# Layer 0 of a four-layer convolution kernel: C spread over the partitions through DRAM, and some events moved to other ticks

## The chip, the core and the metric

The kernel runs on one core of one Trainium2 chip. A core has five engines, each with an instruction stream of its own that it works through in order: TensorE (PE in the profile; PEld are its weight loads), VectorE (DVE), ScalarE (ACT), GpSimd (POOL) and SyncE (SP, which here only issues DMAs). The metric is the device time of one execution in microseconds.

## The reference, cut to what matters

`x` is 8 images of 128 channels and 64 x 64 pixels. Four layers follow, each as `x = x + layer(group_norm(x))`. Only layer 0 is touched. Its upper 64 channels go through a 3 x 3 convolution, its lower 64 through a selective scan over the 4096 pixels of an image:

```
t  = (x_id @ expand_w) @ concat_w + concat_b            # 64 channels
xz = layer_norm(t) @ in_w + in_b;  xs, z = split(xz)    # 128 channels each
xc = silu(causal_conv1d(xs))
dbc = xc @ xproj_w                                      # 4 + 16 + 16 columns
dt = softplus(dbc[:R] @ dt_w + dt_b); B, C = dbc[R:R+16], dbc[R+16:]
h  = exp(dt * A) * h + dt * B * xc                      # scan; h has 128 x 16 states
y  = (sum over the 16 states of h * C + xc * D) * silu(z)
x_id_out = t + y @ out_w + out_b
x = x + relu(concat(x_id_out, conv3x3(x_hw) + conv_b))
```

Layer 1 (`propagate`) is a chain of four directions with 63 steps each, in which a row is added to a 9-tap convolution of the row before. Layers 2 and 3 are a gated convolution and a deformable convolution.

## The kernel before

**Chunks and steps.** `layer0` (L176 on) cuts the 8 images into 32 chunks `c` of 1024 pixels, four an image, and each chunk into two halves `h` of `T` = 512 pixels. A half is scanned in 8 steps `q`, each for 16 of the 128 channels times 8 states, so that a step fills the 128 partitions; the other 8 states are a second column block `k`. There are 512 steps, and the loop over them makes one *tick* a step. In tick i, POOL weighs the step before (`step_weigh`, L771: `carry` L774 and `hb * C` L775), ACT makes the decay of step i + 2 (`da`, L752), DVE makes `ub = u * B` (L760) and the two scans (L769), SP issues the spreads of `u` for step i + 3 and of `dt` for step i + 5 (`u_s`, `dt_s`, L746), and at i % 4 = 1 PE sums four weighed steps over their states (`round_sum`, L784). `da`, `u_s` and `dt_s` have three buffers each, `hb` seven.

**The order of the rest is written out by hand.** `plan_chunk(c)` puts each further operation of a chunk into a tick counted from the chunk's first step, `t0 = 16 c`, with `at` (after the step's own work) or `ahead` (before it). Each engine executes what falls to it in just this order: tick by tick, and within a tick in the order in which the events were planned, lower chunks first. PE's results of this kind share one ring of two PSUM banks (`ps_g`); B has one pair of banks (`B_ps`).

The operations that matter below, with their lines: `t_product` (L448) and `t_var` (L456); `xs_product` (L478), `z_product` (L493); `v_product` (L504) for each half, with ACT's `e` and `rv`; `v_store` (L531), which stores `dt` and `u` to DRAM, from where L746 spreads them; `bc_product` (L535), with a copy by ACT into `bc` (L537); `spread` (L541), a product with a 0/1 matrix that copies 8 rows of `bc` to all 128 partitions, used by `c_spread` (C, then copied by ACT to SBUF at L549) and `b_spread` (B, left in PSUM); `y_product` (L605 and L607, with ACT's L609), the layer's output product; `normalize` (L570), `conv_taps` (L587), the 3 x 3 convolution of the chunk. For the images 4 to 7 this convolution is computed ahead, in the first half of the chunks, with `early_load` (L633), `early_norm` (L639), `conv_taps` into `ps_e`, `early_relu` (L643) and `early_store` (L646) into the DRAM tiles `cd`; `early` shares the single buffer of `bc`. `norm_at` (L325 to L342) takes an image's statistics through two small products, `ps_gn` and `ps_gv`; `norm_x` (L627) normalises an image of layer 1's input in place; `fold` (L404, L408) folds a norm into two biases.

**What runs beside.** From tick 0 on, `borders` (L170, L176) writes zero borders of eight tables, one DMA a tick in the first 64 ticks. From tick `READY` = 282 (c = 17, tick 10 of the chunk) on, each tick also takes one step of `propagate` for the images 0 to 3: nine taps on PE (`ps_l`, L913) and one operation of DVE (L920). From there on the chunks have `beside` set (c > 16), which places a few events differently. When layer 0 has ended, the rest of the propagation runs alone, then `exchange`, and then layers 1 (images 4 to 7), 2 and 3 beside one another.

Of the kernel before, what the change touches and what calls it, by code (L numbers as in the profile page):

```python
# [10 lines left out]
F32 = mybir.dt.float32  # L11
# [6 lines left out]
P = 128  # L18
B, C, H, W = 8, 128, 64, 64
HW = H * W  # L20
NB2 = B // 2

GC, D, DI, N, R, KC = 64, 64, 128, 16, 4, 3
T = 512
# [16 lines left out]
def conv_preact_kernel(ctx: ExitStack, tc: tile.TileContext, a: dict, out: bass.AP):  # L41
    nc = tc.nc
# [4 lines left out]
    dram = ctx.enter_context(tc.tile_pool(name="dram", bufs=1, space=DRAM))  # L47
# [9 lines left out]
        out=gview, in_=gview, pattern=[[-4, 32], [0, 4]], compare_op=ALU.is_ge,  # L57
# [3 lines left out]
        out=gview, in_=gview, pattern=[[4, 32], [0, 4]], compare_op=ALU.is_ge,  # L61
# [8 lines left out]
    x3d = [dram.tile([C, HW], F32, name=f"x3d{b}") for b in range(B)]  # L70
    cd = [dram.tile([P, T], F32, name=f"cd{c}") for c in range(B * HW // (4 * T))]
    wide = {
        name: [dram.tile([P, T], F32, name=f"{name}_{i}") for i in range(B * HW // T)] for name in ("dtd", "ud")
    }
    tables = [dram.tile([SIDE * DEEP, 2 * C], F32, name=f"table{b}") for b in range(B)]

# [1 line left out]
    norm1 = const.tile([P, B, 2], F32, name="norm1")  # L78
    norm2 = {}
    with tc.tile_pool(name="x", bufs=1) as xp, tc.tile_pool(name="l1w", bufs=1) as wd, tc.tile_pool(  # L80
        name="l1ps", bufs=1, space=PSUM
# [15 lines left out]
        st = const.tile([P, B * NCH, 6], F32, name="bn_st")  # L97
        with tc.tile_pool(name="l2w", bufs=1) as wp, tc.tile_pool(name="l2", bufs=2) as w2, tc.tile_pool(
            name="l3", bufs=2
        ) as w3, tc.tile_pool(name="l2ps", bufs=2, space=PSUM) as p2, tc.tile_pool(  # L100
            name="l3ps", bufs=3, space=PSUM
# [23 lines left out]
            for b in range(B):  # L125
                for when, what in sorted(two.plan(b).items()):
                    n = b * two.TICKS + when
                    if b == NB2:
                        n = (b + 1) * two.TICKS - (two.TICKS - 5 - when) // 2
                    plans.setdefault(n, []).extend(what)  # L130
            last = NB2 * two.TICKS + 30
            for n in range(min(plans), (B + 1) * two.TICKS):
                b, i = n // two.TICKS - 1, n % two.TICKS
# [46 lines left out]
def layer0(tc, a, ident, gmat, x_in, x1d, cd, wide, norm1, X, pl):  # L180


    nc = tc.nc
# [3 lines left out]
    with ExitStack() as ctx:  # L187
# [15 lines left out]
        for i in range(4):  # L203
            part = slice(i * HW // 4, (i + 1) * HW // 4)
# [7 lines left out]
        xproj_w = load("xproj_w", [DI, R + 2 * N], (ALL, a["xproj_w"]), pool=tp)  # L212
# [24 lines left out]
        with tc.manual_schedule():  # L237
# [4 lines left out]
            def ps_g(name):  # L242
                return pg.tile([P, T], F32, tag="g", name=name)
# [8 lines left out]
            ps = ps_g("ps_ec")  # L252
# [8 lines left out]
            ps = ps_g("ps_cb")  # L261
# [5 lines left out]
            ps = ps_g("ps_ib")  # L267
# [13 lines left out]
            for i in (1, 2):  # L281
# [3 lines left out]
            ps = ps_g("ps_dt")  # L285
# [3 lines left out]

            w_bc = wp.tile([DI, 4, 32], F32, name="w_bc")  # L290
            nc.gpsimd.memset(w_bc, 0.0)
            nc.vector.tensor_copy(
                w_bc[:, 0:2, 0:8], xproj_w[:, R + N : R + 2 * N].rearrange("p (k n) -> p k n", n=8)
            )
            nc.vector.tensor_copy(w_bc[:, 2:4, 0:8], xproj_w[:, R : R + N].rearrange("p (k n) -> p k n", n=8))
            w_bc = w_bc.rearrange("p j n -> p (j n)")
            n_of = tp.tile([P, 32], F32, name="n_of")
            nc.vector.tensor_copy(n_of, ident[:, 0:32])
            for j in range(1, 4):
# [8 lines left out]
                out=m_y, in_=m_y, pattern=[[128, 2], [-8, 32]], compare_op=ALU.is_ge,  # L308
# [3 lines left out]
                out=m_y, in_=m_y, pattern=[[-128, 2], [8, 32]], compare_op=ALU.is_ge,  # L312
# [4 lines left out]
            w2 = ctx.enter_context(tc.tile_pool(name="l0", bufs=2))  # L317

            def norm_at(when, st, gm, rs, name):

                box = {}

                def gather():
                    mv = box["mv"] = w2.tile([P, 2], F32, name=f"mv_{name}")
                    nc.vector.bn_aggr(mv, st().rearrange("p a s -> p (a s)"))  # L325

                def mean():
                    mv = box["mv"]
                    ps = ps_g("ps_gn")
                    nc.tensor.matmul(ps[:, 0:1], lhsT=gmat, rhs=mv[:, 0:1], start=True, stop=True)  # L330
                    nc.vector.tensor_copy(gm, ps[:, 0:1])
                    dm = box["dm"] = w2.tile([P, 3], F32, name=f"{name}_dm")
                    nc.vector.tensor_sub(dm[:, 0:1], mv[:, 0:1], gm)
                    nc.vector.scalar_tensor_tensor(
                        dm[:, 1:2], dm[:, 0:1], dm[:, 0:1], mv[:, 1:2], ALU.mult, ALU.add
                    )

                def variance():
                    dm = box["dm"]
                    ps = ps_g("ps_gv")  # L340
                    nc.tensor.matmul(ps[:, 0:1], lhsT=gmat, rhs=dm[:, 1:2], start=True, stop=True)
                    nc.vector.tensor_copy(dm[:, 2:3], ps[:, 0:1])  # L342
                    variances.append((dm[:, 2:3], rs))

                for i, f in enumerate((gather, mean, variance)):
                    at(when + i, f)
# [6 lines left out]
            norm0 = {}  # L353
# [16 lines left out]
            def at(when, what):  # L370
                events.setdefault(when, []).append(what)
# [56 lines left out]
            def plan_chunk(c):  # L428
                b, g = c // NCK, c % NCK
                r0 = g * CR  # L430
                t0 = 16 * c
                s = S[c] = {}
# [4 lines left out]
                n0 = norm0.setdefault(b, {})  # L437
# [101 lines left out]
                def spread(h, j, to):  # L539
                    rows = slice(32 * j, 32 * j + 32)  # L540
                    nc.tensor.matmul(to, lhsT=m_bc[rows], rhs=s["bc", h][rows], start=True, stop=True)  # L541

                def c_spread(h):
                    s["C", h] = w2.tile([P, 2, T], F32, name="C")
                    ps = [ps_g("ps_C") for _ in range(2)]
                    for k in range(2):
                        spread(h, k, ps[k])
                    for k in range(2):
                        nc.scalar.copy(s["C", h][:, k], ps[k])  # L549

                def b_spread(h):
                    s["B", h] = pu.tile([P, 2, T], F32, name="B_ps")
# [43 lines left out]
                                s["res"][HI, h], s["ps_c"][sl], AF.Relu, bias=conv_b[sl]  # L596
                            )

                def y_product():
                    n0 = norm0[b]  # L600
                    s["res"] = w2.tile([P, 2, T], F32, name="res", bufs=1)
                    ps = ps_g("ps_o")
                    x = s["xr"][LO, 1 : 1 + CR, :].rearrange("p (h r) w -> p h (r w)", h=2)
                    for h, sl in enumerate((LO, HI)):
                        nc.tensor.matmul(ps[sl], lhsT=n0["ec"][:, 0, :], rhs=x[:, h], start=True, stop=False)  # L605
                    for h, sl in enumerate((LO, HI)):
                        nc.tensor.matmul(ps[sl], lhsT=out_w, rhs=s["y", h], start=False, stop=True)  # L607
                    for h, sl in enumerate((LO, HI)):
                        nc.scalar.activation(s["res"][LO, h], ps[sl], AF.Relu, bias=n0["ec", "b"][sl])  # L609
# [19 lines left out]
                early = {}  # L629
# [9 lines left out]
                    nc.scalar.activation(v, v, AF.Identity, bias=n1["shift"][HI], scale=n1["rs"][HI])  # L639

                def early_relu():
                    early["out"] = w2.tile([P, T], F32, tag="bc", name="early", bufs=1)
                    nc.scalar.activation(early["out"], early["ps_c"], AF.Relu, bias=conv_b)  # L643

                def early_store():
# [17 lines left out]
                def also(f, *args):  # L663
                    return lambda: f(*args)
# [4 lines left out]
                beside = c > total // 2  # L669
# [20 lines left out]
                    at(t0 - 5, z_product)  # L690
                    at(t0 - 5, exps)
                for h in range(2):
                    at(t0 - 18 + (2 if beside else 1) * h, also(v_product, h))
                    for part in range(2):
                        when = t0 - (14 if c == h == 0 else 10) + 6 * h + part
                        at(when, also(v_sum, h, part))
                        at(when + 2, also(v_store, ("dt", "u")[part], h))
                    lead = 12 if c == h == 0 else 0
                    at(t0 - 3 - beside + 8 * h - lead, also(bc_product, h))
                    at(t0 - 1 + 8 * h - lead, also(c_spread, h))  # L700
                    (ahead if beside else at)(t0 + (0 if beside else -1) + 8 * h - lead, also(b_spread, h))
                    at(t0 + 11 + 8 * h, also(y_gate, h))
                at(t0 + 14, also(y_mul, 0))
# [2 lines left out]
                at(t0 - (14 if c else 16), v_round)  # L706
                at(t0 - (12 if c else 15), v_log)
                at(t0 + 14, load_again)
                at(t0 + 22, y_product)
                if b < NB2:  # L710
                    at(t0 + 20, normalize)
                    for j in range(3):
                        at(t0 + 24 + j, also(conv_taps, taps[3 * j : 3 * j + 3]))
                    at(t0 + 27, early_load)
                    at(t0 + 30, early_norm)
                    for j, ks in enumerate((taps[0:3], taps[3:5], taps[5:7], taps[7:9])):
                        at(t0 + 31 + j, also(conv_taps, ks, r0, early))
                    at(t0 + 34, early_relu)
                    at(t0 + 35, early_store)
                else:  # L720
                    at(t0 + 22, conv_load)
                at(t0 + 27, out_add)
# [2 lines left out]
                if b < NB2:  # L725
                    at(t0 + 30, keep_x)
                if g == NCK - 1:
                    norm_at(t0 + 32, lambda: s["st"], norm1[:, b, 0:1], norm1[:, b, 1:2], "n1")
                    if b < NB2:
                        for part in range(4):  # L730
                            at(t0 + 38 + part, also(norm_x, part))


            def where(i):
# [57 lines left out]
            for c in range(total):  # L792
                plan_chunk(c)
                if c % NCK == 0:
                    b = c // NCK
# [636 lines left out]
```

## Time and profile before

| | before |
|---|---|
| three runs, median (lowest to highest) | 6828.69 us (6819.01 to 6831.93) |
| the profiled execution: time, span | 6825.9 us, 6824.2 us |
| mean granted PE clock | 0.877 |
| busy PE, DVE, ACT, POOL | 81%, 62%, 44%, 64% |
| first scan step; propagation begins; layer 0's steps end; propagation of images 0 to 3 ends | 83, 1390, 2617, 2737 us |
| ticks 0 to 281: PE, DVE, ACT, POOL busy of 1300 us | 1010, 1132, 904, 989 us |
| then to 2611 us: of 1221 us | 1198, 953, 589, 787 us |
| 128 copies of C by ACT (L549) | 586 ns each |
| DMA queue q1 (hardware_dynamic) | 300000 packets, 561 MB, 26.9% of 16 engines |

A line of a group or of a timeline names the line of the code, the engine, the operation, and what it writes and reads by the program's names. What stands in brackets at the end of a timeline line is how long the engine was idle before it and what ended that wait. Times in a timeline begin with the start of the span.

### The profile page before, as it was taken

The numbers are of one execution on the slowest core, as the hardware profiler recorded it, in microseconds if no ns is written. First come the engines' busy times: TensorE is split into PE (matmuls) and PEld (weight loads), VectorE is DVE, ScalarE is ACT, GpSimd is POOL, SyncE is SP. The second block draws the span as 40 slices with busy tenths as digits, with TensorE's granted clock in tenths as the row PEclk, the third lists the DMA queues.
The fourth block names the chain that finished last, engine by engine and source line by source line (L and its number), as shares of the span: only waits on it lengthen the run. The fifth ranks groups of instructions, "written<-read, shape, count | busy, mean of one in ns | idle before, by whom it ended". The sixth has DMA issues, their size and how long they took to land. (4 is left out here: it accounts for less than half of the span.)

```text
span 6824.2 us, 76741 instructions
## 1 busy us (share of the span) xinstructions
PE 5519.9 (81%) x25628; PEld 3703.4 (54%) x25628; DVE 4206.7 (62%) x4615; ACT 3000.8 (44%) x5976; POOL 4342.3 (64%) x3758
## 2 busy tenths in 40 slices
PE   4778887799999999899989999977777777876670
PEld 1222222267676767667777777765645555555550
DVE  4889898877777773427677677766542343433235
ACT  4667777655454541313333333333433343433332
POOL 3778787766666662116776776787666666666655
PEclk7777677799999999899999999998888888987775
DMA  4556565544444441525666666667776666676658
GB/s 123 167 173 190 152 182 160 154 133 130 130 130 131 128 132 41 173 80 181 192 191 187 196 191 192 190 178 247 253 223 206 196 212 208 212 213 190 187 164 291
DMA packets 496236, 1195.66 MB, mean 175 GB/s; under 512 B 76248, under 2 KB 117152, under 8 KB 493792
## 3 DMA queue, kind: packets, MB, share of 16 engines
q0 software_dynamic: 184320, 604.13, 30.0%
q1 hardware_dynamic: 300000, 561.43, 26.9%
q10 hardware_dynamic: 11520, 25.18, 1.0%
q8 instruction: 204, 3.34, 0.2%
q14 instruction: 192, 1.57, 0.1%
HBM read 1031.24 MB, written 159.22 MB: 174 GB/s over the span
## 5 line engine op out<-in xcount | busy, mean ns | idle before, releaser
L1264 POOL DMA_INDIRECT got<-table,idx x1614 | 1772.6, 1098 | 1030.1 <-issue 469.4
L913 PE MATMUL ps_l<-X,w_dir 128*128 128x240 f32 (+4 forms) x9072 | 2039.9, 380 | 116.9 <-DVE X L920 75.7
L913 PEld LDWEIGHTS ps_l<-X,w_dir 128*128 128x128 f32 x9072 | 1715.3, 193 | 500.9 <-DVE X L920 186.7
L775 POOL TENSOR_TENSOR hb<-hb,C 128x1024 f32<-128x1024 f32 x512 | 1208.7, 2361 | 41.5 <-POOL carry L774 1.0
L769 DVE TENSOR_TENSOR_SCAN hb<-da,carry,ub_ps 128x512 f32<-128x512 f32 x896 | 1097.8, 1266 | 70.6 <-ACT da L752 13.9
L752 ACT ACTIVATE da<-dt_s,a_neg 128x512 f32<-128x512 f32 x1024 | 678.5, 715 | 569.4 <-DVE hb L769 523.8
L1264 POOL DMA_INDIRECT X<-table,idx x690 | 653.8, 948 | 355.3 <-issue 143.5
L920 DVE SCALAR_TENSOR_TENSOR X<-ps_l,X 128x256 f32<-128x256 f32 x504 | 213.2, 423 | 905.8 <-PE ps_l L913 736.1
L1311 ACT COPY samp<-ps_s 128x384 f32<-128x384 f32 x768 | 365.2, 476 | 860.1 <-remote 455.8
L1304 PE MATMUL ps_s<-ident,got 128*128 128x128 f32 x3594 | 540.9, 295 | 232.1 <-issue 122.7
L1286 ACT ACTIVATE got<-got,wgt 128x128 f32<-128x128 f32 x1614 | 556.7, 400 | 274.7 <-DMA got<-table,idx 220.9
L760 DVE TENSOR_TENSOR ub_ps<-u_s,B_ps 128x1024 f32<-128x1024 f32 x512 | 625.6, 1222 | 82.4 <-PE B_ps L541 52.6
L1317 PE MATMUL ps_o<-samp,dcn_w 128*128 128x256 f32 x2304 | 590.9, 407 | 101.9 <-issue 93.6
L1304 PEld LDWEIGHTS ps_s<-ident,got 128*128 128x128 f32 x3594 | 462.6, 153 | 325.9 <-issue 179.5
L1304 PE MATMUL ps_s<-ident,X 128*128 128x128 f32 x2760 | 424.1, 308 | 187.9 <-issue 166.5
L1317 PEld LDWEIGHTS ps_o<-samp,dcn_w 128*128 128x128 f32 x2304 | 459.7, 204 | 210.5 <-issue 138.5
L774 POOL COPY carry<-hb 128x2 f32<-128x2 f32 x512 | 95.7, 187 | 658.2 <-DVE hb L769 596.4
L1304 PEld LDWEIGHTS ps_s<-ident,X 128*128 128x128 f32 x2760 | 370.9, 161 | 246.8 <-issue 212.3
L1282 DVE TENSOR_TENSOR got<-got,wgt 128x1152 f32<-128x1152 f32 x336 | 453.7, 1351 | 78.0 <-DMA got<-table,idx 70.1
L1297 DVE TENSOR_TENSOR got<-got 128x768 f32<-128x768 f32 x636 | 484.1, 761 | 19.6
L784 PE MATMUL ps_y<-hb,m_y 128*32 128x512 f32 x2048 | 346.2, 742 | 54.4 <-DVE xc L558 41.2
L1282 DVE TENSOR_TENSOR got<-got,wps 128x1152 f32<-128x1152 f32 x202 | 264.4, 1343 | 203.3 <-ACT wps L1278 144.7
(222 smaller groups left out, 6029.8 us busy)
## 6 DMA issues: line engine op xcount, KB each, us to landing
dt_s<-dtd SPq DMA_DIRECT2D x512, 256.0 KB
u_s<-ud SPq DMA_DIRECT2D x512, 256.0 KB
table<-tok SPq DMA_DIRECT2D x128, 256.0 KB
got<-table,idx POOLq DMA_INDIRECT x1614
x<-x2d SPq DMA_DIRECT2D x48, 384.0 KB
x3h<-x3d SPq DMA_DIRECT2D x16, 1056.0 KB
dtd<-dt SPq DMA_DIRECT2D x64, 256.0 KB
ud<-u SPq DMA_DIRECT2D x64, 256.0 KB
```

The costliest lines, as they stand in the source:

```text
L752: nc.scalar.activation(da[:, k], steps[i]["dt"], AF.Exp, scale=a_neg[:, q, k : k + 1])
L760: nc.vector.tensor_mul(ub, st["u"].unsqueeze(1).to_broadcast([P, 2, T]), s["B", h])
L769: nc.vector.tensor_tensor_scan(hb[:, k, :], st["da"][:, k, :], ub[:, k, :], start, ALU.mult, ALU.add)
L775: nc.gpsimd.tensor_mul(hb, hb, S[c]["C", h])
L913: nc.tensor.matmul(ps[:, c0:c1, :], lhsT=w[:, k, :], rhs=v[:, prev, c0 + k - PAD : c1 + k - PAD, :], start=(k == PAD), stop=(k == K - 1),)
L1264: nc.gpsimd.indirect_dma_start(out=got[:, k, :, :].rearrange("p q c -> p (q c)"), out_offset=None, in_=self.tables[b], in_offset=bass.Indi ...
L1282: nc.vector.tensor_mul(got[:, :, 0:3, :], got[:, :, 0:3, :], w.unsqueeze(3).to_broadcast([P, G3, 3, C]))
L1286: nc.scalar.activation(got[:, k, 3, :], got[:, k, 3, :], AF.Identity, scale=wgt[:, t, k0 + k, 3:4])
L1297: self.nc.vector.tensor_add(got[:, :, 0:q, :], got[:, :, 0:q, :], got[:, :, q : 2 * q, :])
L1304: nc.tensor.matmul(ps[:, k, :], lhsT=got[:, k, q, :], rhs=self.ident, is_transpose=True, start=(q == 0), stop=(q == parts - 1),)
L1311: self.nc.scalar.copy(samp[:, k0 : k0 + self.G3, col : col + P], ps)
L1317: nc.tensor.matmul(ps, lhsT=self.dcn_w[:, k, :], rhs=samp[:, k, :], start=(k == 0), stop=(k == KK - 1))
```

## The change

C no longer goes through a product that spreads it and two copies by ACT. `w_bc` is laid out so that the 16 rows of C are rows 0 to 15 of `bc`; `c_store` stores them to a DRAM tile `cs` (16 x 512), and in the next tick `c_spread` reads them back with two broadcasting DMAs, eight rows to 128 partitions each. Both are issued by SP. `bc` is made one tick earlier in the chunks without `beside`.

Other events change their tick: the second `v_product` of a chunk with `beside` one tick earlier; `y_product` is cut in two (`y_start` with the product of `x`, then the product of `y`), and with `beside` the second part comes a tick later; the early convolution's taps, its ReLU and its store one tick later, and `early` has a buffer of its own; for the images 0 to 2, the three parts of the norm of layer 1's input come 4 ticks later and `norm_x` 16 ticks later. The arithmetic stays the same.

```diff
-        name: [dram.tile([P, T], F32, name=f"{name}_{i}") for i in range(B * HW // T)] for name in ("dtd", "ud")
+        name: [dram.tile([n, T], F32, name=f"{name}_{i}") for i in range(B * HW // T)]
+        for name, n in (("dtd", P), ("ud", P), ("cs", N))
...
-            nc.vector.tensor_copy(
-                w_bc[:, 0:2, 0:8], xproj_w[:, R + N : R + 2 * N].rearrange("p (k n) -> p k n", n=8)
-            )
+            nc.vector.tensor_copy(w_bc[:, 0, 0:N], xproj_w[:, R + N : R + 2 * N])
...
+                def c_store(h):
+                    nc.sync.dma_start(wide["cs"][2 * c + h], s["bc", h][0:N])
+
                 def c_spread(h):
                     s["C", h] = w2.tile([P, 2, T], F32, name="C")
-                    ps = [ps_g("ps_C") for _ in range(2)]
                     for k in range(2):
-                        spread(h, k, ps[k])
-                    for k in range(2):
-                        nc.scalar.copy(s["C", h][:, k], ps[k])
+                        source = wide["cs"][2 * c + h][8 * k : 8 * k + 8]
+                        nc.sync.dma_start(s["C", h][:, k], source.unsqueeze(0).to_broadcast([16, 8, T]))
...
-                def y_product():
+                def y_start():
                     n0 = norm0[b]
                     s["res"] = w2.tile([P, 2, T], F32, name="res", bufs=1)
-                    ps = ps_g("ps_o")
+                    ps = s["ps_o"] = ps_g("ps_o")
...
+                def y_product():
+                    n0, ps = norm0[b], s["ps_o"]
                     for h, sl in enumerate((LO, HI)):
                         nc.tensor.matmul(ps[sl], lhsT=out_w, rhs=s["y", h], start=False, stop=True)
...
-                    early["out"] = w2.tile([P, T], F32, tag="bc", name="early", bufs=1)
+                    early["out"] = w2.tile([P, T], F32, name="early", bufs=1)
...
-                    at(t0 - 18 + (2 if beside else 1) * h, also(v_product, h))
+                    at(t0 - 18 + h, also(v_product, h))
...
-                    at(t0 - 3 - beside + 8 * h - lead, also(bc_product, h))
-                    at(t0 - 1 + 8 * h - lead, also(c_spread, h))
+                    at(t0 - 4 + 8 * h - lead, also(bc_product, h))
+                    at(t0 - 3 + 8 * h - lead, also(c_store, h))
+                    at(t0 - 2 + 8 * h - lead, also(c_spread, h))
...
-                at(t0 + 22, y_product)
+                at(t0 + 22, y_start)
+                at(t0 + 22 + beside, y_product)
...
-                        at(t0 + 31 + j, also(conv_taps, ks, r0, early))
-                    at(t0 + 34, early_relu)
-                    at(t0 + 35, early_store)
+                        at(t0 + 32 + j, also(conv_taps, ks, r0, early))
+                    at(t0 + 35, early_relu)
+                    at(t0 + 36, early_store)
...
-                    norm_at(t0 + 32, lambda: s["st"], norm1[:, b, 0:1], norm1[:, b, 1:2], "n1")
+                    delay = 16 if b < NB2 - 1 else 0
+                    norm_at(t0 + 32 + delay // 4, lambda: s["st"], norm1[:, b, 0:1], norm1[:, b, 1:2], "n1")
                     if b < NB2:
                         for part in range(4):
-                            at(t0 + 38 + part, also(norm_x, part))
+                            at(t0 + 38 + delay + part, also(norm_x, part))
```

## The prediction

> **What bounds the kernel now.** The change lies in layer 0, so I first asked what limits layer 0, and read the table of busy time by stretch. Columns: the stretch, its length, then busy time (and instructions) of PE, PEld, DVE, ACT and POOL, then the granted PE clock, DMA share and GB/s.
>
> ```profile
> 90.00:1390.00 1300.00, 1010.09 (x3305) 279.26 (x3304) 1132.28 (x1058) 904.07 (x1266) 989.32 (x765) 0.72 0.58 169
> 1390.00:2611.00 1221.00, 1197.56 (x5681) 851.72 (x5679) 953.32 (x986) 589.31 (x864) 787.08 (x605) 0.99 0.43 129
> ```
>
> There are two stages with different bounds. Up to about 1390 us (ticks 0 to 281) DVE is the fullest engine: 1132 of 1300 us. PE has 1010, but at a mean clock of 0.72. From 1390 to 2611 us layer 1's propagation of images 0 to 3 runs beside the scan, and PE is busy 1197.6 of 1221 us. Until 2737 us the propagation then goes on alone, one step in 4.53 us, so its end sets when all the rest begins. What is saved in either stage reaches the end one to one; after 2737 us the program is unchanged.
>
> Second, for the DVE stage, what DVE waited for (us in total, times, longest):
>
> ```profile
> DVE ub_ps L760 <- PE B_ps L541: 35.2, 16, 6.1
> DVE norm L331 <- PE ps_gn L330: 30.3, 9, 10.2
> DVE ub_ps L760 <- DMA u_s<-ud: 23.5, 7, 4.6
> DVE hb L769 <- ACT da L752: 21.8, 6, 7.5
> DVE ecc_bias L408 <- PE ps_fold L404: 12.5, 4, 3.2
> DVE ec_bias L408 <- PE ps_fold L404: 3.0, 5, 0.7
> ```
>
> These are the stalls that can be won there, some 128 us. Which of them the change touches is seen in the timeline around one start of a chunk (c = 17; starts in us, durations):
>
> ```profile
> 1317.08 1.29 ACT L639 ACTIVATE xa<-xa,norm 64x1088 f32<-64x1088 f32 x1 [0.76 <-DMA xa<-in_x]
> ...
> 1318.41 5.36 PE L587 MATMUL ps_e<-xa,conv 64*64 64x512 f32 x12 [5.88 <-ACT xa L639]
> ...
> 1323.70 1.22 PE L541 MATMUL ps_C<-bc,m_bc 32*128 32x512 f32 x2
> 1323.71 1.22 PE L541 MATMUL B_ps<-bc,m_bc 32*128 32x512 f32 x2
> ...
> 1325.91 1.23 DVE L760 TENSOR_TENSOR ub_ps<-u_s,B_ps 128x1024 f32<-128x1024 f32 x1 [3.60 <-PE B_ps L541]
> ```
>
> PE takes its work in order. At tick 15 it sits idle 5.88 us for the normalised rows of the early convolution, does 5.36 us of its taps, and only then C and B; DVE meanwhile waits 3.60 us for B. Note that C and B start together (1323.70, 1323.71): they use different 32-row groups, so here the C product costs PE nothing of its own.
>
> Third, the PE stage, as a timeline of PE:
>
> ```profile
> 1612.87 1.08 PE L605 MATMUL ps_o<-xr,ec_b 64*64 64x512 f32 x4
> 1613.87 1.08 PE L607 MATMUL ps_o<-xc,out_w 128*64 128x512 f32 x4
> 1614.88 4.02 PE L913 MATMUL ps_l<-X,w_dir 128*128 128x256 f32 x18
> 1618.83 1.13 PE L541 MATMUL ps_C<-bc,m_bc 32*128 32x512 f32 x4
> 1619.89 4.02 PE L913 MATMUL ps_l<-X,w_dir 128*128 128x256 f32 x18
> 1623.84 1.13 PE L541 MATMUL B_ps<-bc,m_bc 32*128 32x512 f32 x4
> ```
>
> Each tick is a propagation step plus what layer 0 has put there. A step alone takes 4.53 us (4.02 and the hand-over to DVE and back); a tick with C 5.01, one with the gated product 5.96, one with B and the second v product 5.97, one with a v product alone 4.72.
>
> **The change, part by part.** *PE stage.* C's product goes from 28 halves (56 of the 128 copies lie there), 1.06 us each. Simply taking it out would give back only 5.01 - 4.53 = 0.48, since the hand-over shows again. But the change refills the slots: the second v product moves from B's tick to C's tick 15, half of the gated product to C's tick 7. Per chunk the four ticks go from 5.96 + 5.01 + 4.90 + 5.97 = 21.84 to 4.97 + 5.00 + 4.72 + 5.01 = 19.70 us, 2.14 less. Thirteen full chunks and some 1.5 for the last: **-29.5**. DVE needs about 4.2 us of such a tick, so it does not take over. Held over two ticks, ps_o makes the second fold product wait for its ACT reads, about 0.7 longer in three chunks: **+2**.
>
> *DVE stage, B at chunk starts.* The early taps move from ticks 15..2 to 0..3, behind B. Twelve waits at c = 2 to 17 sum to 32.2 (1.1 to 6.1 each). Afterwards B (2.1 us at low clock) runs under the two scans (2.45), so about 0.3 each stays: **-28**. The taps now end a tick later; they ended at tick 2.0 to 3.6, and normalize, the next writer of xa, begins on ACT at 4.2 to 4.6. But PE's own wait for early_norm (3.4 to 7.3 a chunk) is gone, which I take to pay for it; ACT works two ticks ahead of the scan.
>
> *norm1's mean* for images 0 to 2 stood in tick 1 behind those taps: waits of 6.1, 4.0, 3.5 (c = 5, 9, 13). In tick 5 it stands behind a round_sum of 1.9 to 3.6 and DVE has 3.7 of scans to do; about 1.5 each may stay: **-9**. The four `norm_x` of 2.24 us each leave the tick of the fold.
>
> *The fold* (c = 5, 9, 13, 17, tick 7) waited for ACT's copies of C, 3.8 us each with its second part, 15.3 in all. With C gone only B is ahead of it: **-12**.
>
> *ACT* loses 128 copies of 0.586 us (75 us) and its waits for C's product (47 in the DVE stage). ACT is on the path only in the prologue: **-1**.
>
> *SP and DMA.* Added are 64 stores of 32 KB and 128 spreads of 256 KB, 0.55 us of issue each, 1.65 a half, on the queue that issues u_s and dt_s. Form and size of a spread are those of u_s, which lands about 3.8 us after its issue. 33.5 MB in 2500 us is 13 GB/s on top of 129 to 169, and the DMA engines are at 0.43 to 0.58. The new wait is SP's, for the store's landing; behind it stand the next u_s and dt_s. No row shows a 32 KB store; the nearest are three 256 KB stores of `early`, awaited by ACT, 3.5, 4.7 and 5.4 us after their issue. The spread comes one tick (3.8 to 5 us) after the store, so SP is held 0 to 1.6 us; u_s is issued over two ticks (some 10 us) ahead and needs 4 to 6. POOL first needs C three ticks after the spread's tick. So in the steady state I cost it at nothing: waits of SP on DVE cover it (341 us in the first stage, 782 in the second); without that cover each us late costs 64 us.
> [...]
>
> The cover is thin while the table borders are written (ticks 0 to 63):
>
> ```profile
> 339.66 0.44 SPq L170 DMA_DIRECT2D table<-X  x1
> 340.19 6.18 SPq L746 DMA_DIRECT2D u_s<-ud  x1
> 346.46 0.55 SPq L746 DMA_DIRECT2D dt_s<-dtd  x1
> ```
>
> The issue behind each L170 write is held 5.3 to 7.3 us, and u_s already comes late eight times (24 us). The new DMAs fall into ticks 5, 6, 13 and 14, just as SP has caught up. Between 0 and 8 x 2.7 = 22 us; nearest to the row that shows SP back on DVE's pace by tick 5: **+4**.
>
> Sum: -29.5 + 2 - 28 - 9 - 12 - 1 + 4 = -73.5. The profiled execution took 6825.9 us (span 6824.2), so 6752; it lies 2.8 below the median shown, 6828.7, and the forecast against that median is **6755**.
>
> **Rivals.**
> 1. *Only PE's part is real (chance 0.2).* The DVE stage's stalls come back elsewhere: in ticks 0 to 3 PE has taps, a round sum, t and its variance, about 24 us at half clock in 15.6 us of ticks; if that is late, normalize holds ACT and DVE waits for `da`. For it: PE is busy 0.78 of that stage, and such `da` waits of 4.5 and 6.4 stand at c = 15, 16. Then -27.5 to -35: about 6797.
> 2. *PE's clock rises (0.1).* PE loses its idle gaps in the first stage, the granted clock (0.72, swinging between 0.5 and 1) rises, and the PE-bound waits that I left in place (10.2 and 3.5 of ps_gn, 4.4 of ps_l, 10.9 of `da`) and my residues (13) go too: up to 40 more, about 6720. The Trainium skill (TensorE: Matmul & The Clock Gate, The HAM clock gate) has the gate close after an idle window of about 3.4 us. The trace agrees in part: at 1318 us PE is at half speed after such a gap, and gaps remain after the change.
> 3. *SP holds the scan: slower (0.1).* C comes through a store, a wait and a spread in SP's single queue. If the store lands later than about 10 us after its issue, u_s behind it is late and DVE waits in each of 64 halves. From there each us costs 64; 1.3 us beyond that point eats the 73 and ends slower, 2 us give about 6885. Against it: 3.5 to 5.4 measured, DMA half idle.
> 4. *Nothing measurable (0.05).* The borders cost the full 22 and rival 1 holds: about 6815.
>
> The forecast has 0.55. **Range 6715 to 6805**: from rival 2 to rival 1 with part of the border price; about 0.17 is left out. The three runs of before lie 0.2% apart, about what a measurement of this kernel can tell from no change. Faster by over 0.2% (below 6815): 0.55 + 0.2 + 0.1, 0.85. Within: 0.05. Slower: 0.10.
>
> **What would show it.** PE stage: a plain chunk of 83.1 instead of 85.2 us, and tick 15 ending in `ps_v`. DVE stage: the wait on B_ps under 8 us, on ps_fold under 4, ps_gn near 20; chunks of 64 to 66 us instead of 66.5 to 78. SP: waits on `DMA cs` below 1.6 us a half; POOL never waiting long for C. It is wrong if DVE's wait on u_s grows beyond 35 us, if `da` or normalize takes the place of B, or if PE idles between propagation steps.

## The result and the profile after

| | before | after |
|---|---|---|
| median of the runs on one chip (lowest to highest) | 6826.16 us (6819.01 to 6831.93) | 6739.74 us (6736.61 to 6746.91) |
| ratio to before, with its 95% interval | | 0.9879 (0.9863 to 0.9894) |
| the profiled execution: time, span | 6825.9, 6824.2 us | 6746.9, 6745.2 us |
| ticks 0 to 281 (from `ub` of step 0 to that of step 282) | 1295.0 us | 1243.6 us, -51.4 |
| from there to the first load of `exchange` | 1358.7 us | 1324.9 us, -33.8 |
| from there to the end | 4087.2 us | 4092.8 us, +5.6 |

The kernel became 86 us faster. The profiled execution is the slowest of the four after; the 5.6 us that it lost behind layer 0, where nothing was changed, do not show in the medians. All the gain lies in layer 0, in both stages. (In this table the first stage ends with tick 281, at 1378 us before; the border at 1390 us, used above, lies 12 us later, and the propagation's products begin at 1387.)

The two stages by busy time (columns as in the prediction; the first stage is now shorter, so the border between the two lines is at 1345 us):

```profile
90.00:1345.00 1255.00, 935.73 (x3181) 267.44 (x3182) 1137.64 (x1062) 870.83 (x1198) 990.37 (x766) 0.74 0.66 191
1345.00:2565.00 1220.00, 1191.98 (x5713) 865.30 (x5711) 956.69 (x995) 558.56 (x804) 791.53 (x607) 1.00 0.49 142
```

DVE has about the same work in the first stage (1138 us, before 1132), in less time; PE has lost 74 us there and is still full in the second. The clock stands where it stood (0.74 after 0.72), and the DMA share rose from 0.58 to 0.66.

What DVE waited for between 90 and 1390 us:

```profile
DVE hb L775 <- ACT da L758: 30.5, 8, 5.8
DVE ub_ps L766 <- DMA u_s<-ud: 28.0, 11, 4.6
...
DVE norm L330 <- PE ps_gn L329: 9.4, 6, 3.4
...
DVE ec_bias L407 <- PE ps_fold L403: 1.1, 4, 0.3
DVE ub_ps L766 <- PE B_ps L540: 1.0, 1, 1.0
```

B went from 35.2 to 1.0 us, ps_gn from 30.3 to 9.4, the fold from 15.5 to 1.3. Waits for `da` and `u_s` grew by 9 and 4.5. Around the start of chunk 17:

```profile
1276.68 1.23 DVE L766 TENSOR_TENSOR ub_ps<-u_s,B_ps 128x1024 f32<-128x1024 f32 x1
1277.96 2.08 PE L540 MATMUL B_ps<-bc,m_bc 32*128 32x512 f32 x4 [5.23 <-DVE ub_ps L766]
1279.97 4.50 PE L587 MATMUL ps_e<-xa,conv 64*64 64x512 f32 x10
1280.59 1.23 DVE L766 TENSOR_TENSOR ub_ps<-u_s,B_ps 128x1024 f32<-128x1024 f32 x1
```

Now PE waits for DVE, not DVE for PE: B starts as soon as `ub` of the step before has freed its banks, is done in 2.08 us under the two scans, and the taps follow. In the PE stage:

```profile
1557.34 1.07 PE L605 MATMUL ps_o<-xr,ec_b 64*64 64x512 f32 x4
1558.35 4.02 PE L919 MATMUL ps_l<-X,w_dir 128*128 128x256 f32 x18
1562.30 1.08 PE L610 MATMUL ps_o<-xc,out_w 128*64 128x512 f32 x4
1563.31 4.02 PE L919 MATMUL ps_l<-X,w_dir 128*128 128x256 f32 x18
1567.25 1.13 PE L540 MATMUL B_ps<-bc,m_bc 32*128 32x512 f32 x4
```

In these ticks one small product stands between two propagation steps. A plain chunk (one without a new image or direction in it) takes 82.9 us where it took 85.2.

### The profile page after: what moved, and what is told of

The parts are those of the page before. It is cut to its first block, busy times and chain, and to the rows that moved or that the text cites. A ratio compares the mean times of both kernels' runs of the same rounds, so it can differ in the third digit from the quotient of the medians.

```text
span 6745.2 us, 76432 instructions
## 1 busy us (share of the span) xinstructions
PE 5399.8 (80%) x25372; PEld 3675.2 (54%) x25372; DVE 4199.4 (62%) x4615; ACT 2946.7 (44%) x5848; POOL 4341.8 (64%) x3758
## 5 line engine op out<-in xcount | busy, mean ns | idle before, releaser
L781 POOL TENSOR_TENSOR hb<-hb,C 128x1024 f32<-128x1024 f32 x512 | 1209.5, 2362 | 59.9 <-DMA C<-cs 18.7
L1310 PE MATMUL ps_s<-ident,got 128*128 128x128 f32 x3594 | 560.0, 299 | 278.5 <-issue 177.0
L766 DVE TENSOR_TENSOR ub_ps<-u_s,B_ps 128x1024 f32<-128x1024 f32 x512 | 625.4, 1221 | 53.5 <-DMA u_s<-ud 28.4
L1323 PE MATMUL ps_o<-samp,dcn_w 128*128 128x256 f32 x2304 | 574.6, 401 | 91.9 <-issue 76.0
L1310 PE MATMUL ps_s<-ident,X 128*128 128x128 f32 x2760 | 409.7, 303 | 170.5 <-issue 148.1
L1339 DVE BATCH_NORM_STATS2 bn_st<-o_out 128x6 f32<-128x512 f32 x64 | 44.0, 687 | 538.9 <-ACT o_out L1333 471.7
```

What stands on the lines that cost most here:

```text
L766: nc.vector.tensor_mul(ub, st["u"].unsqueeze(1).to_broadcast([P, 2, T]), s["B", h])
L781: nc.gpsimd.tensor_mul(hb, hb, S[c]["C", h])
L1310: nc.tensor.matmul(ps[:, k, :], lhsT=got[:, k, q, :], rhs=self.ident, is_transpose=True, start=(q == 0), stop=(q == parts - 1),)
L1323: nc.tensor.matmul(ps, lhsT=self.dcn_w[:, k, :], rhs=samp[:, k, :], start=(k == 0), stop=(k == KK - 1))
```

## The experiments

My theory: the PE stage gains by C's 1.06 us a half only because other products take its slot; the DVE stage gains by B's, the fold's and the norm's waits; the DMAs are free but for the first 64 ticks. The main rivals: one part does it all; SP's wait for the store, or the DMAs' load, costs the scan time.

The same kernels take other times on other chips: the kernel before took 6859 us on the chip of the first four runs, 6866 on that of the next four, 6477 on that of the last three. So I compare ratios to before, and the two stages of layer 0 in microseconds of each profile, which repeat: 1243.6 and 1324.9 for the changed kernel on its first chip, 1238.6 and 1324.8 on the last. By this pair, a difference of some 5 us in the first stage shows nothing. No run undoes the earlier `bc` or the buffer of `early`: what these two are worth by themselves stays open.

| kernel | ticks 0 to 281 | from there to `exchange` | ratio (interval) |
|---|---|---|---|
| before | 1295.0 | 1358.7 | 1 |
| changed | 1243.6 | 1324.9 | 0.9879 (0.9863 to 0.9894) |
| C alone | 1294.4 | 1338.3 | 0.9972 (0.9957 to 0.9987) |
| moves alone | 1262.0 | 1405.2 | 1.0019 (1.0000 to 1.0038) |
| taps back | 1274.3 | 1323.7 | 0.9909 (0.9877 to 0.9941) |
| slots back | 1246.5 | 1338.0 | 0.9895 (0.9865 to 0.9925) |
| norm back | 1242.0 | 1325.1 | 0.9892 (0.9860 to 0.9924) |
| no gap | 1251.0 | 1323.7 | 0.9902 (0.9879 to 0.9926) |
| spreads doubled | 1236.4 | 1326.0 | 0.9875 (0.9850 to 0.9901) |
| borders split | 1208.5 | 1328.3 | 0.9845 (0.9817 to 0.9874) |

**C alone**: the kernel before, with C's new path and these ticks (the edit is abridged).

```diff
-                    at(t0 - 3 - beside + 8 * h - lead, also(bc_product, h))
-                    at(t0 - 1 + 8 * h - lead, also(c_spread, h))      # by PE and ACT
+                    at(t0 - 4 + 8 * h - lead, also(bc_product, h))
+                    at(t0 - 3 + 8 * h - lead, also(c_store, h))
+                    at(t0 - 2 + 8 * h - lead, also(c_spread, h))      # two DMAs
```

> The kernel before with C through DRAM alone (store, spreads, bc one tick earlier without beside); every other event in its old tick. My theory: in the PE stage C's tick falls only from 5.01 to 4.53 us, 28 x 0.48 = -13; the fold's wait for the copies of C goes, -14; the waits for B stay, since the early taps are still ahead of B in tick 15 (above 25 us in all), and so do those for ps_gn. Some -25 to -35 in all, about 6796. Rival (the new path of C is the whole gain and the moves are decoration): -75 or more, 6740 to 6750.

Measured: 0.28% faster (19 us, where 25 to 35 were expected), all of it in the PE stage (-20.4 for the 13 expected); a plain chunk takes 84.3 us, 0.9 less, as expected, and most of the rest is the clock, which stood at half for 14 us of this stage and not for 24. The DVE stage gained nothing, where 14 were expected. The fold's wait fell to 2.5, ps_gn's to 19.7, but B's stayed, and `u_s` and `da` took back 10 and 7 us:

```profile
DVE ub_ps L761 <- PE B_ps L540: 35.7, 16, 6.0
DVE ub_ps L761 <- DMA u_s<-ud: 34.0, 11, 4.7
DVE hb L770 <- ACT da L753: 28.9, 9, 8.5
```

The rival falls. So does my -12 for the fold, as a gain that stands by itself.

**Moves alone**: the changed kernel with C by PE and ACT at its old tick; `bc` stays a tick earlier (the edit is abridged).

```diff
-                    at(t0 - 3 + 8 * h - lead, also(c_store, h))
-                    at(t0 - 2 + 8 * h - lead, also(c_spread, h))      # two DMAs
+                    at(t0 - 1 + 8 * h - lead, also(c_spread, h))      # by PE and ACT
```

> The changed kernel with C spread by PE and copied by ACT again, at its old tick; all moves kept. My theory: the PE stage gains nothing, because the moved products now share their ticks with C (a plain chunk stays at 85 us); in the DVE stage the waits for B go (-28 to -33) and ps_gn's at three chunks (-13), the fold's stay (15). About -40, 6786 (6775 to 6800). Rival (the path of C is the whole gain): no change, 6826.

Measured: no gain; if anything 13 us slower. The DVE stage gained 33, the PE stage lost 46.5. Both parts went otherwise than I had written. In the PE stage the moved product meets C in one tick:

```profile
1639.32 1.13 PE L541 MATMUL ps_C<-bc,m_bc 32*128 32x512 f32 x4
1641.12 1.13 PE L504 MATMUL ps_v<-xc,w_dt 128*128 128x512 f32 x2 [0.67 <-ACT C L549]
1642.08 3.92 PE L918 MATMUL ps_l<-X,w_dir 128*128 128x256 f32 x18
```

C takes both banks of the ring, and the v product stands 0.67 us until ACT has copied one. The gated product does the same to C:

```profile
1504.36 1.12 PE L541 MATMUL ps_C<-bc,m_bc 32*128 32x512 f32 x2
1505.93 1.12 PE L541 MATMUL ps_C<-bc,m_bc 32*128 32x512 f32 x2 [0.46 <-ACT res L612]
1506.98 5.70 PE L918 MATMUL ps_l<-X,w_dir 128*128 128x256 f32 x18
```

The two halves of C, which ran side by side in 1.13 us before, now stand one behind the other with a wait between them, 2.7 us in all. Together the two ticks make a plain chunk 2.3 us longer than before. The rest is mostly the clock: in ten of the fourteen chunks from c = 18 on, the propagation step behind this C ran at half clock for 3.4 us and took 5.70 us for 4.02, some 17 of the 46.5 us.

In the DVE stage the wait for B did *not* go, though the taps were behind it:

```profile
728.86 1.12 PE L541 MATMUL ps_C<-bc,m_bc 32*128 32x512 f32 x2
735.66 1.22 PE L541 MATMUL ps_C<-bc,m_bc 32*128 32x512 f32 x1 [5.68 <-ACT rv L506]
735.67 1.22 PE L541 MATMUL B_ps<-bc,m_bc 32*128 32x512 f32 x2
```

```profile
DVE ub_ps L765 <- PE B_ps L541: 32.6, 16, 4.9
```

The second product of C needs the bank that holds the v product until ACT has read it, and B is queued behind C. At the chunk starts this keeps two thirds of the old wait (22.5 us before tick 282, where it was 33); the rest of the 32.6 stands mostly at tick 8, where C waits in the same way for ACT's read of the gated product. What this stage gained came from ps_gn (30.3 to 10.0), the fold and `u_s`.

**Slots back**: the changed kernel with two products in their old ticks.

```diff
-                    at(t0 - 18 + h, also(v_product, h))
+                    at(t0 - 18 + (2 if beside else 1) * h, also(v_product, h))
-                at(t0 + 22 + beside, y_product)
+                at(t0 + 22, y_product)
```

> The changed kernel with the second v product and the gated product back in their old ticks beside the propagation. My theory: without the refill the hand-over of the propagation shows again, 28 x (1.06 - 0.48) = +16: a plain chunk goes from 82.9 to about 84.2 us, the time to about 6756 (6752 to 6762); the DVE stage is as in the changed kernel. Rival (PE is bound by its total work, so where C's 1.06 us are taken out does not matter): 82.9 us a chunk, 6740.

Measured: +13 us in the PE stage for the 16 expected; a plain chunk takes 84.3 us, as worked out. The rival falls. The hand-over is seen:

```profile
1562.79 1.08 PE L605 MATMUL ps_o<-xr,ec_b 64*64 64x512 f32 x4
1563.79 1.08 PE L610 MATMUL ps_o<-xc,out_w 128*64 128x512 f32 x4
1564.80 4.02 PE L919 MATMUL ps_l<-X,w_dir 128*128 128x256 f32 x18
1569.34 4.02 PE L919 MATMUL ps_l<-X,w_dir 128*128 128x256 f32 x18 [0.52 <-DVE X L926]
```

**Taps back**: the changed kernel with the early taps ahead of B again.

```diff
-                        at(t0 + 32 + j, also(conv_taps, ks, r0, early))
-                    at(t0 + 35, early_relu)
-                    at(t0 + 36, early_store)
+                        at(t0 + 31 + j, also(conv_taps, ks, r0, early))
+                    at(t0 + 34, early_relu)
+                    at(t0 + 35, early_store)
```

> The changed kernel with the early convolution's taps, ReLU and store one tick earlier again, ahead of B in tick 15; early keeps its own buffer. My theory: DVE's wait for B at the chunk starts comes back, +25 to +32 us, about 6768, all of it before tick 282. Rival (B was late because C stood ahead of it and waited for PSUM banks and for bc, so that the taps no longer matter): 6740.

Measured: B's wait is back, and the DVE stage 31 us longer:

```profile
DVE ub_ps L766 <- PE B_ps L540: 37.8, 14, 6.0
```

The rival that C alone had held up B falls. With the two runs above: B had *two* blockers in a row, taps that wait for ACT's `xa`, and C that waits for its banks. With either alone, 32 to 38 us of waiting remain in all; only without both is it 1.0.

**Norm back**: `delay = 0`.

> The changed kernel with the norm of layer 1's input for images 0 to 2 and its norm_x in their old ticks. My theory: ps_gn's waits at c = 5, 9, 13 come back (+10 to +13), and the waits for da at c = 6 and 14 (5.0 and 6.7 us), which I put down to norm_x in the chunk's ticks 6 to 9, go. Net 0 to +5 us, ratio 0.988 to 0.989. Rival (the norm's old place costs more than its wait, through ACT: norm_x beside the fold and the copies): +13 or more, ratio 0.990 or above, with da waits in chunks 5, 9 and 13.

Measured: the two stages of layer 0 are as in the changed kernel (-1.6 and +0.2). The waits on ps_gn came back (22.7 for 9.4), and those for `da` at c = 6 and 14 were gone. My reason for the latter is wrong all the same: in the two runs with other DMAs that follow, `norm_x` stood in its new place, and those waits were absent too (13.8 us for `da` in all); with C alone, where it stood in its old place, they were there at c = 6 and 9. They follow the clock. In the changed kernel's first profile, chunk 6:

```profile
559.00:581.00 22.00, 20.93 (x53) 4.77 (x50) 21.23 (x20) 12.94 (x14) 14.77 (x12) 0.50 0.78 210
```

```profile
580.46 1.38 ACT L595 ACTIVATE res<-ps_c,conv_b 64x512 f32<-64x512 f32 x2 [8.99 <-PE ps_c L587]
```

The taps of that convolution ran wholly at half clock (third column from the right), and ACT, in order, waited 8.99 us for the last of them with `da` behind. Wherever a trace of these kernels has such a wait at tick 14, the taps ended 17 to 21.5 us after tick 8 began; elsewhere they mostly took 11 to 16. So the two profiles of this pair differ in two ways that cancel: 13 us more on ps_gn with the norm back, 13 us less on `da` by the clock. Without the second, the norm's move would be worth some 13 us (an estimate from the two waits); no run shows this by itself, and whether the move has a part in which chunks meet half clock stays open. The rival falls: there is no such wait at c = 5, 9 and 13.

**No gap**: the spreads directly behind the store.

```diff
-                    at(t0 - 2 + 8 * h - lead, also(c_spread, h))
+                    at(t0 - 3 + 8 * h - lead, also(c_spread, h))
```

> The changed kernel with the two spreads of C in the same tick as the store, directly behind it in SP's queue, so that SP stands for the whole landing of the store (3.5 to 5 us by the rows of before) in each of 64 halves, in place of some 0.7 us on average. My theory: SP's waits on DVE and the 10 us by which u_s and dt_s are issued ahead cover it; DVE's wait on u_s grows by less than 15 us, nearly all in the first 64 ticks, and the ratio to before stays at 0.988 to 0.990. Rival 3 of the prediction (what SP is held goes into the scan): 64 x 3 to 4 us = some 200 us, ratio above 1.01.

Measured: SP's wait for the store rose from the first of these lines (changed kernel) to the second (no gap), over all of layer 0:

```profile
SPq L549 <- DMA cs<-bc: 44.6, 32, 3.5
```

```profile
SPq L549 <- DMA cs<-bc: 194.6, 63, 5.8
```

That is 3.1 us in nearly every half, and the scan lost 7 us, all of it in the first 64 ticks (+10; the rest -2.5). The rival that SP's hold goes into the scan falls. DVE's wait on `u_s` grew by 17 us (45.2 for 28.4), not by less than 15, and 9 of them came after the first 64 ticks. This profile also waited 17 us less for `da`, by the clock, so the price of the missing gap may be nearer 17 us than 7.

**Spreads doubled**: two further DMAs of 256 KB a half (abridged).

```diff
+                    for k in range(2):
+                        source = wide["cs"][2 * c + h][8 * k : 8 * k + 8]
+                        again = wide[f"again{k}"][2 * c + h].rearrange("(d n) t -> d n t", n=8)
+                        nc.sync.dma_start(again, source.unsqueeze(0).to_broadcast([16, 8, T]))
```

> The changed kernel with two further DMAs a half, each of the size of a spread of C (256 KB read from the same rows), written to DRAM tiles that nobody reads: the price of the spreads themselves, with SP's issue. My theory: free but for the first 64 ticks, where SP is short of time: 0 to +10 us, ratio 0.988 to 0.990. Rival (the 33.5 MB of spreads load the DMA engines or SP so that u_s, dt_s or C come late everywhere): +30 us or more, ratio above 0.992, with DVE's wait on u_s or ACT's on dt_s spread over all chunks.

Measured: no cost that shows (0.9875). The first 64 ticks took 6 us more; DVE's wait on `u_s` rose by 7 us, 5 of them there, and `da` at c = 6 and 14 was not late this time, which hides it (17 us less). The rival of 30 us or more falls: by the wait on `u_s`, the DMAs as such cost some 7 us. The further ones end in DRAM and not in SBUF, so a price of the writes to SBUF is not covered.

**Borders split**: each border write in two, 64 and 3 rows.

```diff
-            nc.sync.dma_start(
-                tab[:, y0 : y0 + 2, :, :].rearrange("x y s c -> x (y s) c"),
-                zero[0:SIDE].unsqueeze(1).to_broadcast([SIDE, 4, C]),
-            )
+            for lo, hi in ((0, 64), (64, SIDE)):
+                nc.sync.dma_start(
+                    tab[lo:hi, y0 : y0 + 2, :, :].rearrange("x y s c -> x (y s) c"),
+                    zero[lo:hi].unsqueeze(1).to_broadcast([hi - lo, 4, C]),
+                )
```

> The changed kernel with each border write of 67 rows issued as two DMAs, of 64 rows and of 3. My theory: the 5 to 7 us for which the issue behind such a write is held come from its 67 rows (not from its 134 KB, half of u_s's), so with 64 rows they go, and with them the eight late u_s of the first 64 ticks: DVE's wait on u_s falls from 28 to about 5 us, the time by 15 to 23, ratio 0.985. Rival (the hold is the price of its 268 pieces of 512 bytes): no change in the hold, ratio 0.988.

Measured: the hold is gone, from 5 to 7 us to nothing:

```profile
337.68 1.14 SPq L172 DMA_DIRECT2D table<-X  x2
338.93 0.53 SPq L753 DMA_DIRECT2D u_s<-ud  x1
```

```profile
DVE ub_ps L767 <- DMA u_s<-ud: 0.6, 3, 0.2
```

The first 64 ticks take 284 us for 308, and layer 0 is 32 us shorter. That the hold came from the 67 rows, and not from the 268 pieces, is shown by the edit: bytes and pieces are the same. The Trainium skill (DMA: Bandwidth & Descriptors, Why a DMA increments its semaphore by 16 and not by 1) says that a DMA is dealt to the largest number of engines, up to 16, that divides the first dimension of both sides; 67 would leave one. The runs agree with it, though no view here counts the engines.

**ReLU later**: on top of the split borders, the ReLU stands a tick later, and `xs` and `z` of chunks 17 and 18 lie where the chunks before have them:

```diff
-                    if taps[-1] in ks and own is s:
-                        for h, sl in enumerate((HI, LO)):
...
+                def conv_relu():
+                    for h, sl in enumerate((HI, LO)):
...
+                    at(t0 + 27, conv_relu)
-                if beside:
+                if c > total // 2 + 2:
```

> The kernel with split border writes, and two events moved to take ACT out of the waits for da at ticks 13 and 14: the ReLU of the chunk's convolution (ACT waits up to 9 us there for taps at half clock) one tick later, behind the da of that tick; and the products xs and z of chunks 17 and 18, which run before the propagation begins, placed as in the chunks before. My theory: the waits for da fall from 20 to 30 us in the runs so far to about 8 (the start, 5, and a rest), 10 to 15 us less than with the split borders alone, and the chunks no longer depend on which clock the taps met. Ratio to before 0.982 to 0.983. Rival (the da waits come from PE being late, not from ACT's order, so they only move by a tick): as with split borders alone, 0.9845.

On the same chip, the split borders and the changed kernel:

> The kernel with split border writes once more, on the same chip as the kernel with the later ReLU and the changed kernel: ratio to before 0.984 to 0.985 by my theory (the two-part border write is worth 20 to 32 us); 0.988 if the first look was luck.

> The changed kernel itself, on the same chip as the two others, to compare with: ratio to before 0.986 to 0.989, and, since the waits for da at ticks 13 and 14 follow the clock that the convolution's taps meet, other chunks with such waits than in its first profile, 10 to 30 us in all.

Measured: 0.9823 (0.9810 to 0.9837) with the later ReLU, 0.9844 (0.9830 to 0.9857) with split borders, 0.9864 (0.9849 to 0.9879) for the changed kernel. The first two intervals overlap, and layer 0 took 1207.9 + 1329.2 us with the later ReLU, 1205.8 + 1325.0 without: its gain is not shown, although its median is 11 us lower. The half of the edit on chunks 17 and 18 worked: the `da` waits at c = 15 and 16 (4.6 and 5.9) are gone and the two chunks take 128.3 us for 136.5. The half on the ReLU failed: waits of 4.1, 2.4 and 4.7 at tick 14 of c = 6, 8 and 14, where the taps again met half clock; this fits the rival. The split borders beat both kernels of this case. On this chip they were 16 us faster than the changed kernel by the medians, less than the 20 to 32 expected; in the profiles layer 0 is 33 us shorter, and 9 of these are lost behind it, for a reason that no view here shows.

Of the changed kernel I had expected other chunks with late `da` than in its first profile. That was wrong: c = 6, 8, 14, 15 and 16 have them again, 29 us in all. With split borders, one profile has such a wait at c = 6 and the other has not. What decides which chunks meet half clock stays open.

## Why the prediction was right

Forecast 6755, measured 6739.7; -73.5 forecast for the profiled execution's layer 0, -85.2 found. The bounds of both stages and the two mechanisms in the PE stage hold; in the DVE stage the sum came out near in part by luck.

- *PE stage*: -27.5 forecast, -33.8 found. A plain chunk came out at 82.9 for the 83.1 that I had worked out, and the two halves of the argument hold: 0.9 us a chunk without the refill (forecast 0.96), 1.4 more with it. Over thirteen chunks, 2.3 for 2.14 is 2 us. The rest lies mostly in the clock: PE stood at half clock for 24 us of this stage before and for 17 after, worth some 3.4 us (an estimate: half the difference, since at half clock the products shown behind this list take twice as long). Except at the start of the stage, these stretches come where a new direction's `w_dir` is awaited; the waits themselves were the same (11.3 and 11.1 us). The sum had no such term; that it helped is luck. The longer wait of the fold product, +2 in the sum, was 0.5 in each of two chunks.
- *DVE stage*: -46 forecast in all, -51 found. Its waits for B, ps_gn and the fold fell by 69 us, but `da` and `u_s` took back 13, which the sum did not have.
- *B*: -28 forecast, -34 found, but by a reason that was only half of it. "At tick 15 it sits idle 5.88 us for the normalised rows of the early convolution" was one blocker. My remark that C costs PE nothing of its own was true of its time and missed its banks: with C still on PE and the taps out of the way, B kept 32.6 us of waiting.
- *The fold*: -12 forecast, -14 of waiting gone, with C's path as said. Alone it was lost again to other waits.
- *norm1's mean*: -9 forecast; its waits went (13 us), but with the move undone the stage took no longer, in a profile with less waiting for `da`. Not foreseen: ps_gn of image 4 (tick 27) waits 3.4 us for 10.2 (see behind this list).
- *SP, borders*: +4 forecast; the late `u_s` of the borders cost 23.5 us before and after. Steady state: nothing forecast, 4.5 us of late `u_s` found; SP waited 44.6 us in all for the stores, and with 195 the scan was only some 7 to 17 us longer. The nearest rows (3.5 to 5.4 us for a 256 KB store) were close to a 32 KB store, for which SP waited up to 5.8. Single waits reached 3.5 us in the changed kernel, where I had written 0 to 1.6. POOL waited 18.7 us for C, at most 4.3 at a time; that this cost anything is not shown.
- *Rival 1*: `da` grew by 9 us, but at ticks 13 and 14 behind the convolution's taps, not behind `normalize` as the rival has it. *Rival 2* did not come as a whole: the mean clock went from 0.72 to 0.74. *Rival 3* was far off.
- *Signs*: the plain chunk, B_ps (1.0) and ps_fold (1.3) came as written. Three missed: ps_gn fell to 9.4 and not to some 20, the chunks c = 4 to 16 took 65.6 to 71.2 us, not 64 to 66, and single waits for `cs` passed 1.6.

The clock has a share that nobody had planned. ps_gn of image 4 is queued behind the taps of the chunk's convolution, and the same 24 products ran at half clock in the profile before (first line) and at full clock after (second):

```profile
213.55 10.37 PE L587 MATMUL ps_c<-xa,conv 64*64 64x441 f32 x24
211.36 5.30 PE L587 MATMUL ps_c<-xa,conv 64*64 64x441 f32 x24
```

So the 7 us won there are the clock's, as are most of the 9 lost on `da`. The sum had neither; that they nearly cancel is luck.

The sum for B was near because both blockers were removed together. Had the change held only one part, my terms, added one by one, would have said -40 for the moves alone, where +13 was measured.

## What to carry to other kernels

Where an instruction waits at the end of an in-order queue, look for every blocker ahead of it, its time *and* the buffers it asks for: a wait with two causes in series gives up little until both are gone, and terms of a sum are then not additive. Taking work from a full engine pays in full only if other work can take the slot; here each slot between two dependent steps hides 0.5 us of hand-over. The shape of one DMA can hold the whole queue behind it: 67 rows held it for 5 to 7 us, the same rows as 64 and 3 did not. And a wait that differs between two profiles need not come from the edit: look at the granted clock of what it waited for.

## What the runs showed of the hardware

PE can be busy and stay at half clock: 20.93 of 22 us busy at a granted 0.50 in the stretch of chunk 6 with the 64 x 64 taps, where the Trainium skill (TensorE: Matmul & The Clock Gate, The HAM clock gate) lets one busy window of some 3.4 us open the gate. Here the trace disagrees, and "busy" in the profile is no promise of a clock: with the spreads doubled the same 22 us had a mean clock of 0.63, with the norm back 0.69. Nor does the clock fall only after a long idle time: with the moves alone it fell to 0.50 for 3.4 us as the propagation step at 1506.98 began, and in the 18 us before, the longest idle time of PE was 0.46 us. The prediction's rule for the closing of the gate does not explain this one. And small DVE operations can last as long as a POOL multiply beside them: the 128 x 1 step of the norm (L334 before) took 0.22 us at one place and 2.40 at another, where POOL's 2.35 us multiply ran over the same time.
